# Building the count matrices of a graph network: five groups per comparison, from PSUM, with three places for the products

## The chip, the cores and the metric

The kernel runs on one core of a Trainium2 chip. The core has a matrix engine (TensorE, PE in the profile; PEld is its weight load), a vector engine (VectorE, DVE), a scalar engine (ScalarE, ACT), GpSimd (POOL, which here issues the gathers) and SyncE (SP, a queue of DMAs). Matrix products land in PSUM, which has eight banks of 2 KB in each of 128 partitions; all else is in SBUF. Every engine works through its own list in order and waits on semaphores of the others. The metric is the device time of one execution in microseconds.

## The reference

A three-layer graph convolution over 6250 nodes and 100,000 edges (sorted by target), with a residual connection and a layer norm. With self loops added,

```python
deg = segment_sum(1, dst);  dinv = rsqrt(deg)
for W, b in ((W1, b1), (W2, b2), (W3, b3)):        # 256->512, 512->512, 512->256
    h = h @ W
    h = relu(segment_sum(h[src] * (dinv[src] * dinv[dst])[:, None], dst) + b)
return layernorm(x + h)
```

The sum over edges is what costs: it is a product with a sparse 6250 x 6250 matrix of counts.

## The kernel before

Nodes come in 50 blocks of Q = 125. The aggregation of a layer is done block by block of targets, in one of two ways. A *gathered* block reads the rows of its sources from a table in DRAM, 16 chunks of 128 edges, one indirect DMA per chunk (`gather`, line 829, POOL). A one-hot matrix of the targets is compared on DVE, four chunks at a time, against the column numbers that lie in PSUM (`near_cols`, line 798), and a product with it adds the rows into an accumulator (`product`, line 855). Most rows are first split in two halves for a faster product: a cast on ACT (line 870), and the remainder on DVE (line 873). A *dense* block multiplies a 125 x 6250 matrix of edge counts, held as bytes, with the node features in SBUF (`parts`): pieces of it are converted by ACT or DVE (line 806) and go into 50 products (line 898).

Layer 0 takes blocks 0 to 17 dense and 18 to 49 gathered, layer 1 all 50 gathered, layer 2 blocks 0 to 27 dense and 28 to 49 gathered.

The count matrices are made by `counts` (line 688). A block of 125 targets has 25 groups of G = 5 targets, and each group has 128 slots of edges, whose source numbers within a block and keys (source block and target within the group) were laid out by `windows` in `slots`. For a group, DVE compares the 125 column numbers (line 702) and the 250 key numbers (line 704) with the slots' numbers, a product of both one-hot matrices counts the edges into 125 x 250 places of PSUM (`mat_ps`, line 710), and ACT evicts these as bytes into `made` (line 694), two steps and three steps after the comparisons. `mat_ps` is one bank with two halves that take turns. After 25 groups the matrix is stored from `made` to `kept` in DRAM (line 713, by `by_rows`, line 52), and a dense block fetches it from there later (line 720, by line 54). In layer 0 `making_few` makes a matrix and orders its fetch, one matrix after another, 18 in all; layer 1 makes the other ten, spaced 74 chunks apart, each by a generator of its own.

The order of the work is written out by hand. `layer` runs over the chunks. In each it issues the gather, the cast, the remainder and the product of chunks some steps back (the remainder two chunks and the product four chunks behind the gather in layers 0 and 1), then one step of everything in `going` (the work after a block's sum), then one step of each extra generator (`go_fixed`: `windows`, `making_few`, `counts`), then as many dense products as are due. A `yield 1` in a generator means: the next step in the next chunk. The framework adds the semaphores. The gathers of layer 0 go round 19 row buffers (`first_rows[2:]` in `room`), and their targets come free when the product or the split has read them.

Of the kernel before, what the change touches and what calls it, by code (L numbers as in the profile page):

```python
# [21 lines left out]
P = 128  # L22
# [21 lines left out]

EVEN = Q // 16 * 16
# [12 lines left out]
def general_path(ctx: ExitStack, tc: tile.TileContext, x, flat, wts, load_w3, room, out):  # L58
# [9 lines left out]
    w1_sb, w2_sb, w3_sb, b1, b2_sb, b3_sb = wts  # L68
# [22 lines left out]
    nc.scalar.dma_start(out=b1_sb, in_=bass.AP(tensor=b1.tensor, offset=b1.offset, ap=[[0, P], [1, HID]]))  # L91
    agg = const.tile([P, NB, HID], F32, name="agg")
# [280 lines left out]
def sorted_path(ctx: ExitStack, tc: tile.TileContext, x, edges, starts, found, wts, biases, room, late, out):  # L373
# [15 lines left out]
    w1_sb, w2_sb, w3_sb, b3_sb = wts  # L389
    b1, b2_sb = biases  # L390
# [21 lines left out]
    slots = const.tile([P, NW, 2, Q], F32, name="slots")  # L412
# [6 lines left out]
    thr0 = const.tile([P, Q], F32, name="thr0")  # L419
# [5 lines left out]
    def windows(t):  # L425
# [6 lines left out]
        nc.vector.tensor_single_scalar(thr, thr0, float(G * Q * t), op=ALU.add)  # L432
# [58 lines left out]
    with tc.tile_pool(name="sdeg1", bufs=1) as dp1, tc.tile_pool(name="sdeg", bufs=2) as dp, \  # L491
# [25 lines left out]
        thr_i = dp1.tile([P, Q], I32, name="sthr_i")  # L517
# [4 lines left out]
        def numbers():  # L522
# [4 lines left out]
            nc.gpsimd.iota(thr_i, pattern=[[G, Q]], base=0, channel_multiplier=0)  # L527
# [86 lines left out]
        with tc.manual_schedule():  # L614
# [13 lines left out]
            nc.vector.tensor_copy(thr0, thr_i)  # L628
# [20 lines left out]
    made, *used = [room[:Q, n * MW:(n + 1) * MW].bitcast(U8)[:, :NB * Q].rearrange("p (k v) -> p k v", v=Q) for n in range(3)]  # L649
    first_rows = [room[:, at:at + C] for at in range(3 * MW, room.shape[1] - C + 1, C)]  # L650
# [11 lines left out]
    pairs = early.enter_context(tc.tile_pool(name="spairs", bufs=4))  # L662
# [9 lines left out]
    near_cols = ps_cols.tile([P, 512], F32, name="near_cols")[:, :Q]  # L672
    nc.vector.tensor_copy(near_cols, cols[:, :Q])
# [14 lines left out]
    def counts(b, rush=GB + 3):  # L688

        def moved(u):
            nc.scalar.copy(made[:, :, u * G:(u + 1) * G],  # L694
                           mat_ps[:Q, u % 2, :G * NB].rearrange("p (k r) -> p k r", r=G))

        hot = {}
        for u in range(GB + 3):
            if u < GB:
                t, w = divmod(b * GB + u, Q)  # L700
                hot_lo = pairs.tile([P, Q], BF16, name="hot_lo")
                nc.vector.tensor_scalar(hot_lo, hot_cols[:, :Q], slots[:, t, 0, w:w + 1], None, op0=ALU.is_equal)  # L702
                hot_key = pairs.tile([P, G * NB], BF16, name="hot_key")
                nc.vector.tensor_scalar(hot_key, keys, slots[:, t, 1, w:w + 1], None, op0=ALU.is_equal)  # L704
                hot[u] = hot_lo, hot_key
            if u > 2:
                moved(u - 3)
            if 1 < u < GB + 2:
                hot_lo, hot_key = hot.pop(u - 2)
                nc.tensor.matmul(mat_ps[:Q, u % 2, :G * NB], lhsT=hot_lo, rhs=hot_key, start=True, stop=True)  # L710
            if u % rush != rush - 1:
                yield 1
        by_rows(nc.sync, made.rearrange("p k v -> p (k v)"), kept[b], store=True)
# [3 lines left out]
    finished = 0  # L717

# [4 lines left out]
    hot_cols = keys  # L723
# [12 lines left out]
    def layer(i, width, gathered, dense, after, rows, first=0, spacing=1.0, extras=()):  # L736
# [55 lines left out]
        def more_hots():  # L792
            c0 = len(hots) * HOTS
            n = min(HOTS, len(gathered) * (KF + 1) - c0)
            if n > 0:
                at = gathered[0] * (KF + 1) + c0
                hot = onehot.tile([P, HOTS, Q], F32R, name="shot")
                nc.vector.tensor_tensor(hot[:, :n], near_cols.unsqueeze(1).to_broadcast([P, n, Q]),  # L798
# [260 lines left out]
    def making_few():  # L1059

        for m, b in enumerate(few):
            while (b + 1) * GB > seen * Q:
                yield 1
            yield from counts(b) if m else counts(b, 2)
            while finished < m - 1:
                yield 1
            fetch(b, now + 10)

    first = 28
    spacing = (steps(FEW) - first - 12) / FEW  # L1070
    layer(0, C, every[FEW:], few, after1, first_rows, first, spacing, [(0, all_windows()), (1, making_few())])

    def last_weights():
        load_w2()
# [200 lines left out]
```

## Time and profile before

| | us |
|---|---|
| median of 3 runs | 2779.82 (2773.82 to 2794.7) |
| profiled execution | 2769.12 |
| its span | 2767.1 |
| PE busy in the span | 2130.1 (77%) |
| POOL | 1685.0 (61%) |
| DVE | 1512.0 (55%) |
| ACT | 1266.9 (46%) |

The mean granted clock of TensorE was 0.905 of full speed. The busy time of PE is modelled from the starts of its instructions, so 77% is not 77% of its peak. A row of the groups names the line, the engine, the operation, the tile written and those read, the shapes and the number of instructions, then their busy time, the mean of one in ns, and the engine's idle time just before them with what ended most of it. In a timeline the columns are start, duration, engine, line and operation, and in brackets the idle time before and its releaser. "remote" stands for a releaser that the profile cannot name. The durations of one execution are read against that execution; the median of the runs lies 10.7 us above it.

### The profile page before, as it was taken

What the parts mean: (1) busy time and instruction counts of PE and PEld (TensorE: products, weight loads), DVE (VectorE), ACT (ScalarE), POOL (GpSimd) and SP (SyncE); (2) the same over time, 40 slices, a digit from 0 to 9 for tenths busy, and PEclk for the clock granted to TensorE, in tenths of its full rate; (3) what the DMA queues carried; (4) which work ended last, traced back from release to release, by engine and by line L of the source; (5) the groups of instructions that cost most, each with busy time, mean ns of one, the idle gap of its engine ahead of it and who ended that gap; (6) DMA issues with size and microseconds to landing.
All of it is one profiled execution on the core that took longest, in us unless ns stands there. A gap on an engine that the chain in (4) does not pass through costs nothing.

```text
span 2767.1 us, 30455 instructions
## 1 busy us (share of the span) xinstructions
PE 2130.1 (77%) x7965; PEld 1459.2 (53%) x7965; DVE 1512.0 (55%) x3904; ACT 1266.9 (46%) x2777; POOL 1685.0 (61%) x1717
## 2 busy tenths in 40 slices
PE   3367678887878767878778878778787688888886
PEld 2245445555555434545555545545454466666664
DVE  5555445555555355555555555555554255655656
ACT  2445445555555344444444444444444244444443
POOL 2355556666666466667767667676676366566663
PEclk9988889999999888989998889999899789999998
DMA  7344445455445466666767667676676355555553
GB/s 174 92 124 115 134 136 146 123 149 148 126 143 143 123 196 194 203 195 201 211 191 211 186 181 216 195 203 201 182 216 198 98 137 150 142 147 153 151 145 93
DMA packets 178089, 447.70 MB, mean 162 GB/s; under 512 B 43347, under 2 KB 75429, under 8 KB 177904
## 3 DMA queue, kind: packets, MB, share of 16 engines
q0 software_dynamic: 107456, 326.24, 42.1%
q1 hardware_dynamic: 55328, 107.63, 13.5%
q10 hardware_dynamic: 15120, 11.77, 1.7%
q8 instruction: 65, 1.06, 0.2%
q14 instruction: 120, 0.98, 0.1%
HBM read 391.61 MB, written 53.88 MB: 161 GB/s over the span
## 4 chain that ended last, share of the span: by engine, by line
PE 53%; issue 17%; DVE 9%; another core or an unknown queue 7%; ACT 6%; DMA 5%; POOL 3%; ACTq 0%; POOLq 0%; SPq 0%; DVEq 0%
PE sacc L855 20%; PE sacc L898 10%; PE win_ps L985 5%; DMA room<-tab,ssrc 4%; PE win_ps L898 4%; PE mat_ps L898 3%; PE mat_ps L710 3%; PE smm L945 3%; DVE halves L873 3%; ACT halves L870 3%; POOL room L829 2%; PE smm L1002 2%; DVE shot L798 1%; ACT piece L806 1%
## 5 line engine op out<-in xcount | busy, mean ns | idle before, releaser
L829 POOL DMA_INDIRECT room<-tab,ssrc x1664 | 1650.0, 992 | 878.8 <-issue 333.3
L873 DVE TENSOR_TENSOR halves<-room,halves 128x256 fp32r<-128x256 f32 (+1 forms) x1208 | 663.6, 556 | 805.1 <-ACT halves L870 382.7
L855 PE MATMUL sacc<-halves,shot 128*125 128x512 f32 x1808 | 773.3, 486 | 156.0 <-issue 66.0
L870 ACT CAST halves<-room 128x256 fp32r<-128x256 f32 (+1 forms) x1208 | 600.9, 510 | 610.9 <-PE sacc L855 170.0
L855 PEld LDWEIGHTS sacc<-halves,shot 128*125 128x125 f32 x1808 | 349.4, 203 | 494.1 <-issue 289.1
L694 ACT CAST room<-mat_ps 125x250 uint8<-125x250 f32 x700 | 305.6, 437 | 544.2 <-PE mat_ps L710 165.4
L898 PE MATMUL sacc<-parts,piece 125*125 125x512 f32 x1400 | 498.7, 454 | 34.5 <-ACT piece L806 19.4
L855 PE MATMUL sacc<-room,shot 128*125 128x256 f32 (+1 forms) x1120 | 483.9, 516 | 10.6 <-DMA room<-tab,ssrc 10.6
L710 PE MATMUL mat_ps<-hot_key,hot_lo 128*125 128x250 bf16 x700 | 203.4, 291 | 308.3 <-issue 128.5
L898 PEld LDWEIGHTS sacc<-parts,piece 125*125 125x125 f32 x1400 | 254.8, 203 | 274.0 <-issue 196.4
L702 DVE TENSOR_SCALAR hot_lo<-keys,slots 128x125 bf16<-128x125 bf16 x700 | 193.6, 277 | 264.9 <-remote 114.2
L798 DVE TENSOR_TENSOR shot<-near_cols,sdlo 128x500 fp32r<-128x500 f32 x443 | 296.3, 669 | 0.1
L806 ACT CAST piece<-room 125x625 fp32r<-125x625 uint8 x376 | 264.9, 712 | 59.5 <-DVE halves L873 13.0
L855 PEld LDWEIGHTS sacc<-room,shot 128*125 128x125 f32 x1120 | 218.7, 204 | 130.0 <-issue 69.8
L985 PE MATMUL win_ps<-room,w_sb 128*128 128x250 f32 x800 | 218.2, 399 | 6.0 <-ACT room L993 5.3
L704 DVE TENSOR_SCALAR hot_key<-keys,slots 128x250 bf16<-128x250 bf16 x700 | 208.1, 297 | 0.0
L985 PEld LDWEIGHTS win_ps<-room,w_sb 128*128 128x128 f32 x800 | 164.7, 206 | 58.1 <-issue 26.1
L898 PE MATMUL mat_ps<-parts,piece 125*125 125x512 f32 x450 | 132.2, 412 | 16.9 <-ACT piece L806 8.4
L898 PE MATMUL win_ps<-parts,piece 125*125 125x512 f32 x450 | 134.1, 419 | 13.5 <-ACT piece L806 10.3
L710 PEld LDWEIGHTS <-hot_lo 128*125 128x125 bf16 x700 | 104.5, 150 | 60.9 <-issue 24.2
L945 PE MATMUL smm<-w,szt 128*125 128x512 f32 x200 | 110.6, 641 | 1.3 <-DVE st L950 0.6
L1002 PE MATMUL smm<-w,room 128*125 128x256 f32 x400 | 109.0, 398 | 0.0
(174 smaller groups left out, 1246.8 us busy)
## 6 DMA issues: line engine op xcount, KB each, us to landing
room<-kept SPq DMA_DIRECT2D x46, 683.6 KB
room<-tab,ssrc POOLq DMA_INDIRECT x1664
kept<-room SPq DMA_DIRECT2D x28, 683.6 KB
tab<-st SPq DMA_DIRECT2D x75, 224.0 KB
room<-tab SPq DMA_DIRECT2D x50, 224.0 KB
room<-in_x SPq DMA_DIRECT2D x50, 112.0 KB
out<-st ACTq DMA_DIRECT2D x50, 112.0 KB
room<-in_x ACTq DMA_DIRECT2D x4, 1120.0 KB
```

Source lines behind the costliest of these rows:

```text
L694: nc.scalar.copy(made[:, :, u * G:(u + 1) * G], mat_ps[:Q, u % 2, :G * NB].rearrange("p (k r) -> p k r", r=G))
L704: nc.vector.tensor_scalar(hot_key, keys, slots[:, t, 1, w:w + 1], None, op0=ALU.is_equal)
L710: nc.tensor.matmul(mat_ps[:Q, u % 2, :G * NB], lhsT=hot_lo, rhs=hot_key, start=True, stop=True)
L798: nc.vector.tensor_tensor(hot[:, :n], near_cols.unsqueeze(1).to_broadcast([P, n, Q]), dlo.rearrange("p b j -> p (b j)")[:, at:at + n].unsq ...
L806: convert(piece, used[m % 2][:, c * PIECE:(c + 1) * PIECE, :])
L829: nc.gpsimd.indirect_dma_start(out=row, out_offset=None, in_=tables[i], in_offset=bass.IndirectOffsetOnAxis(ap=at, axis=0))
L855: nc.tensor.matmul(acc[:Q, :size], lhsT=hot, rhs=row[:, c0:c0 + size], start=(i == 1 and k == c0 == 0), stop=(k == KF and c0 + size == row ...
L870: nc.scalar.copy(halves[:, :width], landed[chunk - hi_lag])
L873: nc.vector.tensor_sub(halves[:, width:], landed.pop(chunk - lo_lag), halves[:, :width].bitcast(F32))
L898: nc.tensor.matmul(acc_d[:Q], lhsT=got[done // PIECE][:, k % PIECE, :], rhs=parts[:, k], start=False, stop=(k == NB - 1))
L945: nc.tensor.matmul(y_ps, lhsT=zt[:, k, :], rhs=w1_sb[:, k, :], start=(k == 0), stop=(k == KC - 1))
L985: nc.tensor.matmul(h_ps[:, f, :], lhsT=w2_sb[:, k, (f2 + f) * P:(f2 + f + 1) * P], rhs=zt2[:, k, :], start=(k == 0), stop=(k == KH - 1))
```

## The change

`counts` now takes a list of blocks and a list of places, and runs over all their groups as one stream of steps. At every fifth step DVE compares the column numbers of five groups at once (625 elements) and the keys of three (750); two steps later it compares the keys of the other two (500). Both comparisons read the key numbers from PSUM: the tile `near_cols` now holds 250 numbers, of which line 798 still reads the first 125. The product of a group comes at step m + 4 and the eviction at m + 5; within a step the product now stands ahead of the eviction. Products go round three places: the two halves of `mat_ps`, and columns 256 to 505 of the bank of `near_cols`. In layer 0 all 18 matrices are one stream, at two steps a chunk for the first 25 steps, and their evictions go to `made` and `also_made` by turns; fetching is a generator of its own (`fetching_few`), behind `counts` in each chunk. The ten matrices of layer 1 have the one place `made` as before.

To make room, `also_made` is taken from the row buffers of layer 0 (13 are left in turn, of 19), `slots` is kept in bf16, `thr0` is gone (its numbers are computed from `cols` in one instruction, as before), and b3 is no longer loaded at the start but after layer 1, by a DMA in SP's queue.

```diff
-    slots = const.tile([P, NW, 2, Q], F32, name="slots")
+    slots = const.tile([P, NW, 2, Q], BF16, name="slots")
...
-        nc.vector.tensor_single_scalar(thr, thr0, float(G * Q * t), op=ALU.add)
+        nc.vector.tensor_scalar(thr, cols[:, :Q], float(G), float(G * Q * t), op0=ALU.mult, op1=ALU.add)
...
-    made, *used = [room[:Q, n * MW:(n + 1) * MW].bitcast(U8)[...] for n in range(3)]
-    first_rows = [room[:, at:at + C] for at in range(3 * MW, room.shape[1] - C + 1, C)]
+    made, *used, also_made = [room[:Q, n * MW:(n + 1) * MW].bitcast(U8)[...] for n in range(4)]
+    first_rows = [room[:, at:at + C] for at in range(4 * MW, room.shape[1] - C + 1, C)]
...
-    pairs = early.enter_context(tc.tile_pool(name="spairs", bufs=4))
+    pairs = early.enter_context(tc.tile_pool(name="spairs", bufs=2))
...
-    near_cols = ps_cols.tile([P, 512], F32, name="near_cols")[:, :Q]
-    nc.vector.tensor_copy(near_cols, cols[:, :Q])
+    near = ps_cols.tile([P, 512], F32, name="near_cols")
+    near_cols = near[:, :G * NB]
+    nc.vector.tensor_copy(near_cols, keys)
+    mat_places = [mat_ps[:Q, 0, :G * NB], mat_ps[:Q, 1, :G * NB], near[:Q, 256:256 + G * NB]]
...
-    def counts(b, rush=GB + 3):
-        def moved(u):
-            nc.scalar.copy(made[:, :, u * G:(u + 1) * G],
-                           mat_ps[:Q, u % 2, :G * NB].rearrange("p (k r) -> p k r", r=G))
+    def counts(blocks, places, rush=0):
+        def compared(out, numbers):
+            shape = list(out.shape)
+            nc.vector.tensor_tensor(out, near_cols[:, :shape[2]].unsqueeze(1).to_broadcast(shape),
+                                    numbers.unsqueeze(2).to_broadcast(shape), op=ALU.is_equal)
 
         hot = {}
-        for u in range(GB + 3):
-            if u < GB:
-                t, w = divmod(b * GB + u, Q)
-                hot_lo = pairs.tile([P, Q], BF16, name="hot_lo")
-                nc.vector.tensor_scalar(hot_lo, hot_cols[:, :Q], slots[:, t, 0, w:w + 1], None, op0=ALU.is_equal)
-                hot_key = pairs.tile([P, G * NB], BF16, name="hot_key")
-                nc.vector.tensor_scalar(hot_key, keys, slots[:, t, 1, w:w + 1], None, op0=ALU.is_equal)
-                hot[u] = hot_lo, hot_key
-            if u > 2:
-                moved(u - 3)
-            if 1 < u < GB + 2:
-                hot_lo, hot_key = hot.pop(u - 2)
-                nc.tensor.matmul(mat_ps[:Q, u % 2, :G * NB], lhsT=hot_lo, rhs=hot_key, start=True, stop=True)
-            if u % rush != rush - 1:
-                yield 1
-        by_rows(nc.sync, made.rearrange("p k v -> p (k v)"), kept[b], store=True)
+        total = len(blocks) * GB
+        for s in range(total + 5):
+            if s < total and s % GB == 0:
+                while (blocks[s // GB] + 1) * GB > seen * Q:
+                    yield 1
+            if s < total and s % WIDE == 0:
+                t, w = divmod(blocks[s // GB] * GB + s % GB, Q)
+                hot_lo = pairs.tile([P, WIDE, Q], BF16, name="hot_lo")
+                hot_key = pairs.tile([P, WIDE, G * NB], BF16, name="hot_key")
+                hot[s // WIDE] = hot_lo, hot_key
+                compared(hot_lo, slots[:, t, 0, w:w + WIDE])
+                compared(hot_key[:, :3], slots[:, t, 1, w:w + 3])
+            if s < total and s % WIDE == 2:
+                t, w = divmod(blocks[s // GB] * GB + s % GB + 1, Q)
+                compared(hot[s // WIDE][1][:, 3:], slots[:, t, 1, w:w + WIDE - 3])
+            m = s - 4
+            if 0 <= m < total:
+                hot_lo, hot_key = [h[:, m % WIDE] for h in hot[m // WIDE]]
+                nc.tensor.matmul(mat_places[m % 3], lhsT=hot_lo, rhs=hot_key, start=True, stop=True)
+            m = s - 5
+            if 0 <= m:
+                n, u = divmod(m, GB)
+                place = places[n % len(places)]
+                nc.scalar.copy(place[:, :, u * G:(u + 1) * G], mat_places[m % 3].rearrange("p (k r) -> p k r", r=G))
+                if u == GB - 1:
+                    by_rows(nc.sync, place.rearrange("p k v -> p (k v)"), kept[blocks[n]], store=True)
+                    stored.append(blocks[n])
+            if s >= rush or s % 2:
+                yield 1
...
-    def making_few():
+    def fetching_few():
         for m, b in enumerate(few):
-            while (b + 1) * GB > seen * Q:
-                yield 1
-            yield from counts(b) if m else counts(b, 2)
-            while finished < m - 1:
+            while b not in stored or finished < m - 1:
                 yield 1
             fetch(b, now + 10)
...
-    layer(0, C, every[FEW:], few, after1, first_rows, first, spacing, [(0, all_windows()), (1, making_few())])
+    layer(0, C, every[FEW:], few, after1, first_rows, first, spacing, [(0, all_windows()), (1, counts(few, (made, also_made), GB)), (1, fetching_few())])
...
-          extras=[(5, last_weights())] + [(10 + gap * n, counts(b)) for n, b in enumerate(many[FEW:])])
+          extras=[(5, last_weights())] + [(10 + gap * n, counts([b], (made,))) for n, b in enumerate(many[FEW:])])
     there.clear()
     fetch(many[0], 6)
     early.close()
+    b3_sb = ctx.enter_context(tc.tile_pool(name="slate_bias", bufs=1)).tile([P, C], F32, name="sb3")
+    nc.sync.dma_start(out=b3_sb, in_=bass.AP(tensor=b3.tensor, offset=b3.offset, ap=[[0, P], [1, C]]))
```

## The prediction

> **What bounds the kernel now.** I read the windows by stage first, since the three layers have different limits (layer 0 97 to 950 us, layer 1 953 to 2185, layer 2 2185 to 2767). Columns: stretch, length, then PE, PEld, DVE, ACT, POOL busy, granted clock, DMA share, GB/s.
>
> ```profile
> 97.00:950.00 853.00, 652.72 (x2572) 451.62 (x2572) 445.01 (x1476) 431.62 (x1041) 504.34 (x520) 0.91 0.46 130
> 953.00:2185.00 1232.00, 964.91 (x3351) 620.60 (x3351) 679.07 (x1413) 539.55 (x1075) 819.36 (x806) 0.90 0.68 195
> 2185.00:2767.00 582.00, 479.99 (x1845) 360.83 (x1845) 335.18 (x879) 262.56 (x598) 345.26 (x355) 0.91 0.52 138
> ```
>
> PE leads everywhere, and in layer 0 it idles 853.0 - 652.7 = 200 us. The groups of that stage say before which instruction:
>
> ```profile
> L710 PE MATMUL mat_ps<-hot_key,hot_lo 128*125 128x250 bf16 x450 | 130.9, 291 | 177.9 <-issue 60.8 <-DVE hot_key L704 53.5 <-ACT room L694 45.0
> ```
>
> 177.9 of the 200 us lie before L710, the counting product that the change rewrites. The releasers named disagree, so I read the timeline of an ordinary stretch:
>
> ```profile
> 706.54 0.27 PE L710 MATMUL mat_ps<-hot_key,hot_lo 128*125 128x250 bf16 x1
> ...
> 706.84 0.44 ACT L694 CAST room<-mat_ps 125x250 uint8<-125x250 f32 x1 [0.35 <-issue]
> ...
> 707.34 0.27 PE L710 MATMUL mat_ps<-hot_key,hot_lo 128*125 128x250 bf16 x1
> ...
> 709.34 0.43 ACT L694 CAST room<-mat_ps 125x250 uint8<-125x250 f32 x1 [1.48 <-PE sacc L855]
> ...
> 709.82 0.27 PE L710 MATMUL mat_ps<-hot_key,hot_lo 128*125 128x250 bf16 x1 [1.31 <-issue]
> ```
>
> Each product starts 0.05 us after the eviction of the product before it ends (706.84 + 0.44 + 0.05 = 707.34; 709.34 + 0.43 + 0.05 = 709.82), though that eviction reads the other half of mat_ps. In all 449 pairs of layer 0 none starts earlier. So mat_ps acts as one place, and PE and ACT go in lockstep: product, eviction, product. Eviction and next product are issued in the same step, so PE has no slack for a late ACT. The second stall is at the end of a matrix:
>
> ```profile
> 279.68 0.43 ACT L694 CAST room<-mat_ps 125x250 uint8<-125x250 f32 x1 [3.27 <-PE sacc L855]
> ...
> 280.13 0.75 SPq L52 DMA_DIRECT2D kept<-room  x2
> ...
> 294.51 0.43 ACT L694 CAST room<-mat_ps 125x250 uint8<-125x250 f32 x1 [12.92 <-remote]
> ...
> 295.00 0.37 PE L710 MATMUL mat_ps<-hot_key,hot_lo 128*125 128x250 bf16 x1 [13.85 <-DVE hot_key L704]
> ```
>
> The next matrix's first eviction waits until the store of the last has left `made`, and PE stands 13.85 us (mostly 2 to 4 us elsewhere). Summed from the timeline: 58 us in layer 0 at the second product of a matrix, 118 us at 87 other products; of the 118, 38 us is in excess of 1.5 us a gap.
>
> Layer 1 by the same view, with counting, without, with, without:
>
> ```profile
> 1192.00:1234.80 42.80, 31.56 (x121) 20.32 (x119) 26.78 (x74) 22.02 (x51) 27.38 (x28) 0.92 0.62 175
> 1234.80:1305.90 71.10, 59.08 (x196) 37.17 (x196) 39.09 (x68) 28.86 (x53) 50.62 (x50) 0.93 0.73 214
> 1305.90:1344.10 38.20, 28.59 (x116) 18.78 (x115) 25.70 (x70) 22.29 (x49) 28.72 (x27) 0.96 0.70 201
> 1344.10:1411.30 67.20, 56.74 (x199) 37.89 (x199) 36.93 (x64) 29.06 (x54) 47.36 (x47) 0.90 0.71 206
> ```
>
> Per gather (POOL's count): 42.8/28 = 1.53 and 38.2/27 = 1.41 us with, 71.1/50 = 1.42 and 67.2/47 = 1.43 without. Over all ten matrices I find 1.59 against 1.44: 27 steps x 0.15 x 10 = 41 us is all that counting costs there.
>
> **The change, part by part.** *Comparisons.* Rows:
>
> ```profile
> L702 DVE TENSOR_SCALAR hot_lo<-keys,slots 128x125 bf16<-128x125 bf16 x700 | 193.6, 277 | 264.9 <-remote 114.2
> L798 DVE TENSOR_TENSOR shot<-near_cols,sdlo 128x500 fp32r<-128x500 f32 x443 | 296.3, 669 | 0.1
> L704 DVE TENSOR_SCALAR hot_key<-keys,slots 128x250 bf16<-128x250 bf16 x700 | 208.1, 297 | 0.0
> ```
>
> The old pair overlaps: 0.44 us from the first's start to the second's end in the timeline, so 2.2 us for five groups. The new ones are shaped like L798, 669 ns at 500 elements; with the 1260-element comparison of the setup (1464 ns) the slope is 1.05 ns. So 625 elements 0.80, 750 0.93, 500 0.67: 2.40 us. DVE gains 140 x 0.2 = 28 us of work. The Trainium skill (VectorE: DVE Perf Modes, the perf-mode tier table) speaks against this part: 16-bit single-source operations in SBUF run at 4x, a two-source one with a PSUM operand at 1x. By the page's cycle table the old pair costs about 0.22 us, 1.1 for five, and the new ones 2.3: 170 us more DVE work by the rule, 28 by the rows. I take the rows. DVE is busy 445 of 853 us, which hides either; uncovered, 28 us is the price. What isn't averaged away: 0.80 + 0.93 = 1.73 us now stand in one step ahead of later `halves`, which PE needs two chunks (3 us) later. Covered.
>
> *Lead and places.* Compared inputs are two to four steps old rather than two: no gain by itself. Products go to three places, two in the old bank and one in the bank of near_cols; product before eviction within a step. A product into the old bank now waits for an eviction issued a step earlier, 1.5 us of slack. Of the 118 us that leaves the 38 us of excess, so 80 us could go; but PE then meets the next late thing (`halves`, `piece`: layer 2, which has no counting, still idles 102 of 582 us). I take 40.
>
> *Two places for matrices.* The store has 25 steps (40 us) to finish. The 58 us go; I take 50, as some of it will surface in front of L855. Half-clock pieces of 3.4 us follow 11 of these stalls; without them PE saves 11 x 1.7 = 19 at most, I take 10. The store itself and the fetch behind it stay in SP's queue, ahead of the same stores of `tab`; nothing there moves but the load of b3, from the start to after layer 1, behind the first fetch and ahead of after3's loads: 0 to 3 us, I take 1.
>
> *The new wait.* The trace says a bank is one place; the Trainium skill (PSUM, Partial Sum Buffer: PSUM bank collisions raise a hardware error) says the same for any two engines, disjoint columns and reads included. By that rule the third place isn't free: every third product must wait for all DVE reads of near_cols issued before it (comparisons and L798), and these for it, as must ACT's eviction. Behind the waiting product stand PE's L898 and L855; behind a waiting comparison DVE's `halves`. No row shows it. Lower bound 0: DVE now finishes a step's comparisons 1.5 us (median) before the product of the same step. Upper bound: the DVE work of the same step in full, 1.73 us at one of five such products, 0.67 at another, L798's 0.67 at about a quarter: 0.66 us each, 99 us for 150 products in layer 0, 55 for 83 in layer 1. A gain is excluded: it only adds waits. I take a third, because DVE's median lead nearly covers the long pair: 33 and 18.
>
> *The rest.* Gather rows in layer 0 fall from 19 to 13. Layer 1 runs on 11 with rows twice as wide; POOL stands 128 us in layer 0 because it is a full 19 ahead. 0 to 15 us, I take 3. Setup loses an iota and a copy: -1. `slots` in bf16, `thr` from cols: same instructions, 0.
>
> Sum, layer 0: -40 - 50 - 10 + 33 + 3 = -64. Layer 1: of the 41 us the product itself needs some 6; of 35 I take -33, then + 18: -15. With b3 and setup 0: **-79 us**. The profiled execution took 2769.1 (span 2767.1), so 2690; it lies 11 below the median of 2779.8, so against the median: **2701 us**.
>
> **The rivals.** (1) *Only the store stall goes* (0.17): the lockstep with ACT is replaced by one with DVE of the same cost; -58 to -30, about 2740. For it: no bank is spare. Against: only every third product meets DVE. (2) *The bank of near_cols decides* (0.17), slower: PE, DVE and ACT chained through it, `halves` behind comparisons that wait for PE, PE's L855 behind these. It outweighs the gain of about 133 us (100 in layer 0, 33 in layer 1) from 133/233 = 0.57 us for each third product; at 0.8 us it gives +53, about 2833. For it: the upper bound of 0.66 counts only one step's DVE work. Against: DVE's idle half. (3) *No change* (0.11), 2780: the late completions before the evictions (709.34, where ACT and DVE alike were waiting for PE) belong to PE itself and move to L855, and the store gain is eaten by (2). (4) *Forecast* (0.55), 2640 to 2750.
>
> **How the numbers follow.** A difference of 1% (28 us) is about what this kernel's measurement tells from none. Faster 0.55 + 0.17 = 0.72, same 0.11, slower 0.17. Low end 2645: all of the 80 and 58, the clock's 19, layer 1's 35, half the coupling taken: -135. High end 2800: it takes in no change and the milder part of (2). The forecast's own range is 2645 to 2750.
>
> **What would show it.** Right: idle before the counting product in layer 0 falls from 178 to under 90 us; no eviction waits for a store; layer 0 shortens by some 65 us, layer 1 by some 15; comparisons near 0.80, 0.93 and 0.67 us. Wrong: gaps of over 1 us before every third product, released by a comparison or L798; DVE idle before comparisons, released by L710; more idle before L855 for `halves`. A layer 0 that is no shorter with the gaps gone would mean PE's own late completions.

## The result and the profile after

| | before | after |
|---|---|---|
| median, measured side by side, us | 2784.9 (4 runs, 2773.82 to 2794.7) | 2747.05 (4 runs, 2741.93 to 2759.55) |
| profiled execution, us | 2769.12 | 2741.93 |
| its span, us | 2767.1 | 2740.3 |

The ratio is 0.985, with a 95% interval of 0.9806 to 0.9894: 38 us less, where 79 were forecast. The direction is as predicted, the size is not. The two profiled executions, which the windows and rows below come from, differ by 27 us.

The windows of the changed kernel by layer, columns as before (stretch, length, then PE, PEld, DVE, ACT, POOL busy, granted clock, DMA share, GB/s):

```profile
97.10:927.50 830.40, 641.88 (x2572) 440.47 (x2572) 462.48 (x847) 416.23 (x1041) 502.62 (x521) 0.90 0.47 134
927.50:2158.20 1230.70, 962.78 (x3351) 616.21 (x3351) 689.30 (x1063) 532.01 (x1075) 808.35 (x805) 0.90 0.67 195
2158.20:2740.30 582.10, 485.82 (x1845) 364.75 (x1845) 339.18 (x879) 263.46 (x598) 346.54 (x355) 0.90 0.52 138
```

In these two executions everything was gained in layer 0, 856 to 830 us (64 were forecast, 26 came). Layer 1 took 1231 us before and takes 1231 (15 were forecast). PE's idle time in layer 0, length less busy, went from 203 us (taken to 953 us) to 830.4 - 641.9 = 188.5: only 15 less, though the counting product lost far more. The groups of layer 0 in the changed kernel say where the rest is:

```profile
L963 PE MATMUL smm<-w,szt 128*125 128x512 f32 x200 | 110.0, 640 | 24.9 <-DVE st L968 15.7 <-DVE shot L816 5.4 <-DVE halves L891 2.7
L721 PE MATMUL mat_ps<-hot_key,hot_lo 128*125 128x250 bf16 x300 | 86.3, 290 | 35.3 <-ACT room L726 25.1 <-ACT halves L888 7.7 <-issue 2.4
L721 PE MATMUL near_cols<-hot_key,hot_lo 128*125 128x250 bf16 x150 | 45.9, 306 | 68.2 <-DVE hot_key L699 40.3 <-issue 15.6 <-DVE shot L816 5.8
L939 PE MATMUL szt_ps<-ident_r,szs 125*128 125x125 f32 x100 | 20.4, 286 | 17.1 <-ACT szt L957 9.2 <-issue 4.3 <-ACT piece L824 1.9
```

Two things are to be seen. The idle time before the counting product fell from 177.9 to 35.3 + 68.2 = 103.5 us, and two thirds of it now lie before the third of the products that go to the third place, with the long comparison as the releaser. And the products of `after1`, the work behind a block's sum (lines 963 and 939, before them 945 and 921), now wait 24.9 and 17.1 us, where they waited 1.3 and 2.1:

```profile
L945 PE MATMUL smm<-w,szt 128*125 128x512 f32 x200 | 110.6, 641 | 1.3 <-DVE st L950 0.6 <-ACT szt L939 0.5 <-issue 0.2
L921 PE MATMUL szt_ps<-ident_r,szs 125*128 125x125 f32 x100 | 19.6, 278 | 2.1 <-DVE szs L932 1.7 <-ACT szt L939 0.4
```

The executions fell into two settings of the hardware, whose cause the profile doesn't name: in one the kernel before took 2763 to 2785 us in median (A; "the first chip" of the expectations), in the other 2351 to 2352 us (B, "the second chip"), so ratios are compared within a setting only; the result above and the profile that the prediction read are of A.

### The profile page after: what moved, and what is told of

The parts are those of the page before. It is cut to its first block, busy times and chain, and to the rows that moved or that the text cites. A ratio compares the mean times of both kernels' runs of the same rounds, so it can differ in the third digit from the quotient of the medians.

```text
span 2740.3 us, 29549 instructions
## 1 busy us (share of the span) xinstructions
PE 2122.7 (77%) x7965; PEld 1447.4 (53%) x7965; DVE 1543.6 (56%) x2923; ACT 1245.0 (45%) x2777; POOL 1673.3 (61%) x1716
## 3 DMA queue, kind: packets, MB, share of 16 engines
q8 instruction: 65, 1.06, 0.2%
## 4 chain that ended last, share of the span: by engine, by line
PE 47%; issue 16%; DVE 8%; ACT 6%; another core or an unknown queue 5%; DMA 3%; POOL 2%; ACTq 0%; SPq 0%; DVEq 0%; POOLq 0%
PE sacc L873 19%; PE sacc L916 9%; PE win_ps L1003 4%; PE win_ps L916 3%; PE mat_ps L916 3%; ACT halves L888 3%; DMA room<-tab,ssrc 3%; DVE halves L891 3%; PE smm L1020 2%; PE smm L963 2%; DVE hot_key L699 2%; POOL room L847 2%; DVE shot L816 1%; ACT piece L824 1%
## 5 line engine op out<-in xcount | busy, mean ns | idle before, releaser
L916 PE MATMUL sacc<-parts,piece 125*125 125x512 f32 x1400 | 505.3, 453 | 40.6 <-ACT piece L824 19.3
L726 ACT CAST room<-mat_ps 125x250 uint8<-125x250 f32 x470 | 197.2, 436 | 304.8 <-PE mat_ps L721 119.6
L699 DVE TENSOR_TENSOR hot_key<-near_cols,slots 128x750 bf16<-128x750 f32 (+1 forms) x280 | 224.1, 801 | 37.9 <-remote 16.1
L726 ACT CAST room<-near_cols 125x250 uint8<-125x250 f32 x230 | 100.7, 438 | 197.3 <-DVE hot_key L699 65.3
L721 PE MATMUL mat_ps<-hot_key,hot_lo 128*125 128x250 bf16 x470 | 134.4, 288 | 68.6 <-ACT room L726 35.8
L721 PE MATMUL near_cols<-hot_key,hot_lo 128*125 128x250 bf16 x230 | 70.2, 305 | 140.4 <-DVE hot_key L699 62.8
L699 DVE TENSOR_TENSOR hot_lo<-near_cols,slots 128x625 bf16<-128x625 f32 x140 | 113.1, 808 | 54.3 <-PE sacc L873 14.6
```

The lines of the kernel that those rows point to most:

```text
L699: nc.vector.tensor_tensor(out, near_cols[:, :shape[2]].unsqueeze(1).to_broadcast(shape), numbers.unsqueeze(2).to_broadcast(shape), op=ALU. ...
L721: nc.tensor.matmul(mat_places[m % 3], lhsT=hot_lo, rhs=hot_key, start=True, stop=True)
L726: nc.scalar.copy(place[:, :, u * G:(u + 1) * G], mat_places[m % 3].rearrange("p (k r) -> p k r", r=G))
L916: nc.tensor.matmul(acc_d[:Q], lhsT=got[done // PIECE][:, k % PIECE, :], rhs=parts[:, k], start=False, stop=(k == NB - 1))
```

## The experiments

### The same two kernels again

No edit.

> The kernel before unaltered, for a profile on the same chip. Idle before its counting product: with the second matrix place alone it was 47 us in layer 0 and 69 us in layer 1; the store stall should add 17 gaps of 2 to 5 us, so 80 to 120 us in layer 0, if the second place is worth anything; 55 if the stall is covered.

> The changed kernel unaltered, so that it can be set beside the experiments on their chip (where the kernel before takes 2352 us, not 2785, and products complete without the late releases). The forecast's mechanism (waits removed before the counting product, less the new wait in the bank of near_cols) says a ratio of 0.97 to 0.99 here too. If the bank of near_cols costs what two places alone saved, it is slower than the kernel with two places (0.9897): 1.00 to 1.03.

> The changed kernel unaltered, beside the three below on one chip. Two chips have served so far: on one the kernel before takes about 2770 to 2785 us, on the other 2352. On the first a ratio of 0.9855 again. On the second, where products complete without late releases and the lockstep with ACT costs less: 0.99-1.02, since the bank of near_cols costs the same and there is less to gain; above 0.9897, the ratio of the kernel with two places there.

In A the changed kernel again took 0.9855 of the time before (0.9816 to 0.9894; medians 2727.25 and 2767.09). By a second profile of each (the kernel before took 2770.11 us in it), layer 0 went from 857 to 821 us, layer 1 from 1229 to 1225. So two executions of one kernel differ by up to 10 us in a layer, and the gain is stable. In B the changed kernel is slower: 1.0046 (1.003 to 1.0062; 2363.72 against 2350.95). A change that gains 1.5% in one setting and loses 0.5% in the other holds terms of both signs. The next runs take them apart.

### The second place for matrices, taken away

```diff
-    (1, counts(few, (made, also_made), GB))
+    (1, counts(few, (made,), GB))
```

> The changed kernel, but all matrices of layer 0 are evicted to the one place made. Theory (the store of the last matrix held the first eviction of the next, 58 us of idle before the product in layer 0, and the second place is the larger part of the gain): 2780-2800, gaps of 2 to 5 us back at the start of each of 17 matrices. Rival (with the places and the lead a store of 5 us is mostly covered): 2747-2760.

> The changed kernel with the one place made in layer 0, as e2. On the second chip 1.04 again. On the first: if the second place is worth the 50 us of the prediction, 1.003 (0.9855 + 0.018); if the stall without it grows to 6 us and more at each of 17 matrices because PE, DVE and ACT all hang on the bank, 1.02 or more.

> The changed kernel with the one place made in layer 0, a third time; wanted on the first chip. There: 1.003 if the second place is worth the predicted 50 us within the changed kernel; 1.02 or more if PE, DVE and ACT all hang on the bank of near_cols while the eviction waits for the store. On the second chip 1.04 again.

In A: 1.0023 (0.9994 to 1.0053), layer 0 back at 858 us. All the rest of the change together is worth nothing there. In B: 1.0395 (1.0372 to 1.0418) and 1.0379 (1.0348 to 1.041). The waits of layer 0 (columns: sum, number, longest, in us) show ACT's eviction waiting for the store again, in the run in A

```profile
ACT room L726 <- DMA kept<-room: 74.7, 15, 9.3
```

and in the second of those in B:

```profile
ACT room L726 <- DMA kept<-room: 82.0, 17, 9.5
```

The changed kernel with both places has no such row. Layer 0 of the second run in B, and of the changed kernel in B:

```profile
96.80:886.10 789.30, 630.08 (x2572) 436.31 (x2572) 461.64 (x847) 417.37 (x1041) 501.77 (x521) 0.92 0.48 141
96.80:809.10 712.30, 607.23 (x2572) 419.63 (x2572) 460.75 (x847) 417.02 (x1041) 504.18 (x520) 0.97 0.53 156
```

It grew by 789 - 712 = 77 us, about the 82.0 us of waiting. Not all of that is idle time of PE: 54 us are, and the other 23 are busy time of PE for the same instructions, at a granted clock of 0.92 instead of 0.97.

### The second place alone, put into the kernel before

```diff
-    made, *used = [... for n in range(3)]
-    first_rows = [room[:, at:at + C] for at in range(3 * MW, ...)]
+    made, *used, also_made = [... for n in range(4)]
+    first_rows = [room[:, at:at + C] for at in range(4 * MW, ...)]
...
-    def counts(b, rush=GB + 3):
+    def counts(b, rush=GB + 3, made=made):
...
-            yield from counts(b) if m else counts(b, 2)
+            yield from counts(b, made=(made, also_made)[m % 2]) if m else counts(b, 2)
```

> The kernel before with the second place for matrices in layer 0 alone (13 row buffers); comparisons, places of the products and their order as before. If the second place is worth what the prediction took (50 us): 2725-2745, and the changed kernel's other parts cancel. If the idle moves to other products: 2765-2785.

> The kernel before with the second place for matrices alone. On the first chip: the prediction took 50 us for it (0.982). On the second chip it gave 0.9967, so the stall of the store alone is mostly followed by another wait; if the same holds on the first chip, 0.99-1.00.

In A: 0.9889 (0.983 to 0.9948), layer 0 at 814 us, 43 less than before. By the ratio that is 31 us, most of the whole change's 38 to 40, for four edited lines. In B: 0.9967 (0.9953 to 0.998), 8 us. The counting product in layer 0 of this kernel, in A:

```profile
L710 PE MATMUL mat_ps<-hot_key,hot_lo 128*125 128x250 bf16 x450 | 131.0, 291 | 142.2 <-issue 60.0 <-ACT room L694 29.0 <-DVE hot_key L704 26.6
```

36 us of idle time before it went, and PE's idle time in the whole layer fell by nearly as much, 203 to 170 us (length less busy in the row below): this gain did not move elsewhere. PE's busy time fell too, from 653 us (in both profiled executions of the kernel before) to 643.

```profile
97.10:910.80 813.70, 643.32 (x2572) 447.43 (x2572) 443.88 (x1476) 431.77 (x1041) 507.27 (x520) 0.92 0.48 137
```

The products of `after1` hardly waited in it:

```profile
L945 PE MATMUL smm<-w,szt 128*125 128x512 f32 x200 | 105.6, 614 | 2.4 <-DVE st L950 1.2 <-issue 0.6 <-ACT szt L939 0.5
L921 PE MATMUL szt_ps<-ident_r,szs 125*128 125x125 f32 x100 | 20.3, 286 | 1.5 <-DVE szs L932 1.1 <-ACT szt L939 0.2 <-issue 0.2
L842 PE MATMUL sacc<-parts,ident_r 125*125 125x512 f32 x32 | 14.9, 465 | 1.4 <-DVE szs L932 1.4
```

### The third place, taken away

```diff
-    mat_places = [mat_ps[:Q, 0, :G * NB], mat_ps[:Q, 1, :G * NB], near[:Q, 256:256 + G * NB]]
+    mat_places = [mat_ps[:Q, 0, :G * NB], mat_ps[:Q, 1, :G * NB]]
...
-                nc.tensor.matmul(mat_places[m % 3], ...)
+                nc.tensor.matmul(mat_places[m % 2], ...)
```

(and `m % 2` in the eviction).

> The changed kernel, but products take turns in the two halves of mat_ps alone; nothing is counted into the bank of near_cols. Theory A (the wait between PE and DVE in the bank of near_cols is what took the missing gain: 68 us before that product in layer 0, 72 us in layer 1): those waits vanish and do not come back elsewhere, layer 0 falls from 830 to 780-805 us, layer 1 by 10 to 30, the whole to 2690-2725. Rival B (DVE is late in any case, and PE would wait for it at another instruction): idle moves to L855 and the products after a block's sum, the whole within 10 us of the changed kernel's 2747. Rival C (three places are what gives the slack): idle before the product rises above the changed kernel's 103 us in layer 0, the whole above 2760.

> The changed kernel with the products in the two halves of mat_ps alone, as e1. On the first chip: with narrow comparisons two places cost 18 thousandths against three (0.9924 and 0.9742), because the slack of the third hides late releases; but here the long comparisons leave PE's path with the third place. If the wait in the bank of near_cols is the larger: 0.975-0.985, faster than the changed kernel; if the third place's slack is: 0.99-1.00. On the second chip 0.99 again.

> The kernel with two places and long comparisons, a third time; wanted on the first chip (the kernel before at about 2770). There: if the wait in the bank of near_cols is the larger cost, 0.975-0.985; if the slack of the third place against late releases is, 0.99-1.00. On the second chip 0.99 again.

In A: 0.9867 (0.9812 to 0.9923), the same as with three places. In B: 0.9897 (0.988 to 0.9913) and 0.9916 (0.9886 to 0.9946), against 1.0046 with three, measured beside the second of these: there the third place costs 2363.72 - 2332.17 = 31.5 us. Layer 0 in B with three places,

```profile
L721 PE MATMUL mat_ps<-hot_key,hot_lo 128*125 128x250 bf16 x300 | 83.7, 282 | 2.8 <-ACT room L726 2.7
L721 PE MATMUL near_cols<-hot_key,hot_lo 128*125 128x250 bf16 x150 | 44.5, 297 | 50.7 <-DVE hot_key L699 42.6 <-DVE shot L816 6.5 <-ACT room L726 0.8
```

and with two:

```profile
L721 PE MATMUL mat_ps<-hot_key,hot_lo 128*125 128x250 bf16 x450 | 125.1, 278 | 21.7 <-ACT room L726 19.3
```

With three places the wait for ACT's eviction falls from 19.3 to 2.7 us. (That is not the third place's doing alone: with three places and the comparisons out of the bank, two sections on, it is 20.7.) In its stead come 50.7 us before the products of the third place, 49 of them released by DVE's reads of that bank. Layer 0 is 712 us with three places and 680 with two. The Trainium skill (PSUM, Partial Sum Buffer: PSUM bank collisions raise a hardware error) asks that two engines be kept apart by bank, not by column; the columns here are disjoint, and the products waited all the same. The waits are for semaphores, which the framework sets; no run here shows what the chip would do without them.

### Old comparisons with three places, and with two

The changed kernel with the comparisons of before, group by group from SBUF, but still four steps ahead; `slots` in F32, seven pairs of buffers:

```diff
-            if s < total and s % WIDE == 0:
+            if s < total:
...
-                compared(hot_lo, slots[:, t, 0, w:w + WIDE])
-                compared(hot_key[:, :3], slots[:, t, 1, w:w + 3])
...
+                nc.vector.tensor_scalar(hot_lo, keys[:, :Q], slots[:, t, 0, w:w + 1], None, op0=ALU.is_equal)
+                nc.vector.tensor_scalar(hot_key, keys, slots[:, t, 1, w:w + 1], None, op0=ALU.is_equal)
```

The kernel with two places has the edit of the section above as well.

> The changed kernel, but comparisons of one group at a time from SBUF as before (lines 702 and 704 of the kernel before; slots in float32), four steps ahead; three places, the third in the bank of near_cols. Theory A (long comparisons in the bank are what PE waits for): the third place's product now waits for L798's comparison alone, idle before it in layer 0 under 30 us, ratio 0.985-0.995. Rival (five groups at once save DVE time and so the wait): slower than the changed kernel.

> Narrow comparisons from SBUF, three places, as e5. On the first chip 0.974 again. On the second: if the long comparisons in the bank are the cost there too, faster than the changed kernel by 1% or more; if comparing five groups at once saves time there (DVE is busy 64% of the span), slower than the kernel with two places (0.9897).

> As e5, with the products in the two halves of mat_ps alone. If the gain of the two-place kernel (0.9897) comes from the lead and from the product standing ahead of the eviction, and not from comparing five groups at once: 0.985-0.993. If the comparisons from PSUM carry it: 0.995 or more.

In A: 0.9742 (0.9702 to 0.9782; 2697.92 us) with three places, 0.9924 (0.9891 to 0.9958; 2744.55 us) with two. In B, with three: 0.9926 (0.9897 to 0.9954). The four kernels that have both places for matrices, ratio to before in A (0.9867 has its own runs of the kernel before, the others share theirs):

| | two places for products | three |
|---|---|---|
| comparisons group by group, from SBUF | 0.9924 | 0.9742 |
| five groups at once, from PSUM | 0.9867 | 0.9855 |

With the old comparisons the third place is worth 2744.55 - 2697.92 = 47 us; with the long ones in its bank, by the ratios, 3 us, give or take 19. The long ones show no cost with two places (0.9867 against 0.9924), and cost 2727.25 - 2697.92 = 29 us with three (B: 2363.72 - 2334.16 = 30 us). So it is neither the comparisons' length nor the third place that costs, but that they meet in one bank. The kernel with old comparisons and three places beats both kernels of this case in both settings.

Its groups in layer 0, in A (lines lie three below those of the changed kernel, so 960, 936 and 857 are 963, 939 and 860 there):

```profile
L960 PE MATMUL smm<-w,szt 128*125 128x512 f32 x200 | 109.7, 638 | 14.2 <-DVE st L965 6.8 <-DVE shot L813 3.3 <-issue 2.2
L718 PE MATMUL mat_ps<-hot_key,hot_lo 128*125 128x250 bf16 x300 | 85.7, 288 | 61.3 <-ACT room L723 31.8 <-issue 22.5 <-ACT halves L885 5.4
L718 PE MATMUL near_cols<-hot_key,hot_lo 128*125 128x250 bf16 x150 | 43.2, 288 | 19.8 <-DVE shot L813 13.8 <-issue 5.2 <-ACT room L723 0.8
L936 PE MATMUL szt_ps<-ident_r,szs 125*128 125x125 f32 x100 | 20.9, 292 | 30.6 <-ACT szt L954 16.9 <-ACT halves L885 5.7 <-issue 3.8
L857 PE MATMUL sacc<-parts,ident_r 125*125 125x512 f32 x32 | 14.8, 462 | 14.2 <-DVE szs L947 10.2 <-issue 3.0 <-PE sacc L913 1.0
```

Its layer 0:

```profile
96.80:899.60 802.80, 631.57 (x2572) 440.09 (x2572) 430.70 (x1477) 413.03 (x1041) 507.37 (x521) 0.92 0.48 139
```

Here the long comparisons are gone, and yet PE's idle time in layer 0 is 802.8 - 631.6 = 171.2 us, as in the kernel before with the second place alone (813.7 - 643.3 = 170.4); the 11 us by which the layer is shorter lie in PE's busy time. Before the counting product it is 61.3 + 19.8 = 81.1 us instead of 142.2, so 61 us went; before the three other lines above it is 59.0 us, where that kernel had 2.4 + 1.5 + 1.4 = 5.3, so 54 us came back. Line 857, the first product into an accumulator, waits there for `after1` to have read the bank. By these sums lead and third place moved PE's waits in layer 0 to `after1`; they did not remove them. The sums don't say why `after1` is now late: PE may reach its products sooner, or the new order of steps may hold up its evictions, and no run changed `after1` alone.

The same is seen with long comparisons and two places, in A:

```profile
L721 PE MATMUL mat_ps<-hot_key,hot_lo 128*125 128x250 bf16 x450 | 128.8, 287 | 98.6 <-issue 50.7 <-ACT room L726 42.6 <-ACT halves L888 1.5
L963 PE MATMUL smm<-w,szt 128*125 128x512 f32 x200 | 110.0, 639 | 18.6 <-DVE st L968 11.8 <-issue 3.7 <-DVE halves L891 1.6
L860 PE MATMUL sacc<-parts,ident_r 125*125 125x512 f32 x32 | 14.6, 456 | 12.7 <-DVE szs L950 12.7
```

44 us less than 142.2 before the counting product, and layer 0 took 814 us, as with the second place alone.

### The long comparisons, but from SBUF

```diff
-            nc.vector.tensor_tensor(out, near_cols[:, :shape[2]].unsqueeze(1).to_broadcast(shape),
+            nc.vector.tensor_tensor(out, keys[:, :shape[2]].unsqueeze(1).to_broadcast(shape),
```

> The changed kernel, but the comparisons of five groups read the key numbers from SBUF (the tile keys, bf16), so of DVE only L798's comparison reads the bank of near_cols. Theory A: waits of the third place's product for hot_key vanish (63 us in both layers), the whole 2690-2725. Rival B: PE waits for the inputs or for halves instead, within 10 us of 2747. The duration of a comparison tells what the PSUM operand costs: near 0.8 us for 625 elements if only the element rate counts, about 0.45 if a 16-bit SBUF operand doubles it; if two SBUF inputs hold POOL up, POOL's gather grows beyond 984 ns.

1.0154 (1.0136 to 1.0172) in B, slower than the changed kernel there. The run was to free the bank and leave all else. It did free the bank of the long comparisons. Before the products of the third place in layer 0,

```profile
L721 PE MATMUL near_cols<-hot_key,hot_lo 128*125 128x250 bf16 x150 | 42.6, 284 | 20.5 <-DVE shot L816 15.3 <-ACT room L726 5.0
```

20.5 us of waiting are left of 50.7, and the 42.6 us that a comparison had ended are gone, though the comparisons are as long as before: that wait came from the bank, and not from the products' inputs. But the run did not leave all else. The products into `mat_ps` wait 21.0 us instead of 2.8. Two rows over the whole kernel, shapes kept apart,

```profile
L847 POOL DMA_INDIRECT room<-tab,ssrc x1664 | 1694.0, 1018 | 508.1 <-issue 225.1 <-DMA room<-tab,ssrc 82.0 <-DVE halves L891 53.3
L699 DVE TENSOR_TENSOR hot_lo<-keys,slots 128x625 bf16<-128x625 bf16 x140 | 113.2, 808 | 10.0 <-PE mat_ps L721 8.2 <-PE near_cols L721 1.7
```

and the gathers of the changed kernel in B:

```profile
L847 POOL DMA_INDIRECT room<-tab,ssrc x1664 | 1644.6, 988 | 538.0 <-issue 247.8 <-DMA room<-tab,ssrc 65.0 <-DVE halves L891 54.9
```

The comparisons hardly wait any more (10.0 us), but a gather takes 1018 ns instead of 988 (in layer 0, 1049 instead of 963). So this kernel's time doesn't tell the price of the bank, as another cost came in; the runs with two places do. Which of the new waits made it slower was not taken apart.

### Layer 1 with a fifth of its counting

```diff
-    def counts(blocks, places, rush=0):
+    def counts(blocks, places, rush=0, groups=None):
...
-            if s < total and s % WIDE == 0:
+            if s < total and s % WIDE == 0 and (groups is None or s < groups):
...
-          ... (10 + gap * n, counts([b], (made,)))
+          ... (10 + gap * n, counts([b], (made,), groups=5))
```

(and the same condition at the second comparison, the product and the eviction).

> The changed kernel; in layer 1, 20 of the 25 groups of each of the ten matrices are left out (no comparison, product or eviction; the store stays), so the counts of blocks 18 to 27 are not the graph's. What layer 1 pays for counting. If the 0.15 us a step of the prediction is on the path: layer 1 shorter by 25-40 us on the first chip, 5-10 on the second. If layer 1 is set by its gathers and splits, and slower steps while counting are made up for in between: under 10 us on both, as the idle before L873 grows by what goes before the product.

0.9799 (0.9728 to 0.987) in A. Layer 1 by its window:

```profile
921.80:2120.50 1198.70, 967.36 (x3151) 600.36 (x3151) 605.11 (x943) 475.32 (x875) 813.47 (x805) 0.90 0.69 201
```

1199 us, 26 to 32 less than the changed kernel's 1225 and 1231, for four fifths of the counting: all of it would cost 33 to 40 us. The medians of the whole kernel agree with that but don't pin it down: 0.9799 against 0.9855 is 16 us, give or take 22. The prediction had worked out 41 from the gathers' pace. So by the profiles there was about that much to gain in layer 1, and the change gained little or none of it (1231 and 1225 us, where it had been 1231 and 1229). Its own groups of layer 1 show why:

```profile
L873 PE MATMUL sacc<-halves,shot 128*125 128x512 f32 x1200 | 504.7, 509 | 143.5 <-ACT halves L888 73.5 <-issue 54.6 <-DVE halves L891 12.2
...
L721 PE MATMUL mat_ps<-hot_key,hot_lo 128*125 128x250 bf16 x170 | 48.1, 284 | 33.3 <-issue 15.4 <-ACT room L726 10.6 <-ACT halves L888 7.2
```

The 33.3 us before the products into `mat_ps` are joined by 72.2 us before the 80 into the third place: 105 together, where there were 130 before the change. And as much as left, and a little more, has come before line 873. The same two groups of layer 1 before the change:

```profile
L855 PE MATMUL sacc<-halves,shot 128*125 128x512 f32 x1200 | 507.3, 509 | 117.4 <-issue 64.6 <-ACT halves L870 36.4 <-DVE halves L873 9.2
...
L710 PE MATMUL mat_ps<-hot_key,hot_lo 128*125 128x250 bf16 x250 | 72.6, 290 | 130.4 <-issue 67.7 <-ACT room L694 21.8 <-DVE hot_key L704 21.7
```

With the counting nearly gone line 873 (874 in this kernel) waits longer still:

```profile
L874 PE MATMUL sacc<-halves,shot 128*125 128x512 f32 x1200 | 528.8, 521 | 195.4 <-ACT halves L889 85.9 <-issue 80.7 <-DVE halves L892 24.6
```

Of some 93 us of idle time taken from the counting product, 52 came back there.

## Why the prediction was half right

The runs in A split the time as the prediction split it (ratios times 2767 us):

| step | predicted, us | measured, us | by |
|---|---|---|---|
| second place for matrices, with the clock's part and the rows | -50 - 10 + 3 | -31 (interval -47 to -14) | put in alone; taken out: -47 |
| lead and places, layer 1's part with them | -40 - 33 | -41, give or take 20; -18 by the spans of the profiles | 0.9889 to 0.9742 |
| the wait in the bank of `near_cols` | +33 + 18 | +31, give or take 16 | 0.9742 to 0.9855 |
| sum | -79 (with b3 and setup at 0) | -41 | up to rounding the ratio 0.9855 itself, so it doesn't confirm the split; the first measurement gave -38 |

**The step that failed** is the size of the second row: 32 of the 39 us that are missing. (The first row is short by 26 us put in alone, by 10 taken out; the third cost 20 us less than allowed.) The prediction said of the lockstep's 118 us: "80 us could go; but PE then meets the next late thing (`halves`, `piece`: ...). I take 40", and of layer 1's 35: "I take -33". The direction of the first sentence was right, and half was still far too much. Without the long comparisons 61 us did leave the counting product in layer 0, and 54 returned before the next late thing. That was not `halves` or `piece` of that stage, but the products around `after1`, which wait for short evictions of ACT and DVE (`szt`, `st`, `szs`). By the profiles, layer 0 with old comparisons and three places is 11 us shorter than with the second place alone, and layer 1 12 us, against 40 and 33; what the medians gain beyond that (41 against 18 us) these two profiles don't show. That the measured 2747 us lie inside the forecast's own range of 2645 to 2750 is luck as far as this split goes.

**The new wait** has its sign, its place and its mechanism as predicted, and a size in time (31 of 51) within the bounds. Its idle time was larger than foreseen, 68.2 + 72.2 us instead of 33 + 18, and in layer 1 above the upper bound of 55; but much of that stands in the place of waits that PE had anyway. The gaps lie in the steps that were named: of the third-place products of layer 0 those of every fifth (the pair of 1.73 us) waited 0.93 us on average, another fifth (the 0.67 us comparison) 0.72 us, the other three fifths 0.21 us; in the second execution in A it was 0.73, 1.06 and 0.25. "DVE's median lead nearly covers the long pair" did not hold. The lead was read in a kernel in which DVE had nothing to wait for in that bank (and it is 1.3 us in median in that trace's layer 0, not 1.5); now the comparisons themselves wait for PE and ACT. The timeline of the changed kernel, where a pair and a third-place product share a step (rows of other work between them left out):

```profile
664.90 0.81 DVE L699 TENSOR_TENSOR hot_lo<-near_cols,slots 128x625 bf16<-128x625 f32 x1 [1.76 <-PE sacc L873]
665.62 0.93 DVE L699 TENSOR_TENSOR hot_key<-near_cols,slots 128x750 bf16<-128x750 f32 x1
...
666.61 0.32 PE L721 MATMUL near_cols<-hot_key,hot_lo 128*125 128x250 bf16 x1 [3.16 <-DVE hot_key L699]
```

The pair starts after 1.76 us of waiting for PE and ends at 665.62 + 0.93 = 666.55, and the product, whose own inputs were compared five steps earlier, starts 0.06 us later.

**The comparisons** cost what the rows had said, 0.80, 0.93 and 0.67 us predicted. By shape, in the changed kernel:

```profile
L699 DVE TENSOR_TENSOR hot_key<-near_cols,slots 128x750 bf16<-128x750 f32 x140 | 129.9, 928 | 0.0
L699 DVE TENSOR_TENSOR hot_lo<-near_cols,slots 128x625 bf16<-128x625 f32 x140 | 113.1, 808 | 54.3 <-PE sacc L873 14.6 <-ACT room L726 13.2 <-PE near_cols L721 9.8
...
L699 DVE TENSOR_TENSOR hot_key<-near_cols,slots 128x500 bf16<-128x500 f32 x140 | 94.2, 673 | 37.9 <-remote 16.1 <-ACT room L726 7.2 <-issue 4.0
```

DVE's busy time rose from 1512.0 to 1543.6 us, by 32 where 28 were predicted. The choice of the rows over the rule was right. The rule's estimate of 0.22 us for the old pair left out what the Trainium skill says beneath that cycle table (VectorE: DVE Perf Modes, The TRN2 errata), that the fixed part measures about 150 cycles and not 58: with that the estimate is 0.41 us, near the 0.44 of the trace.

**The second place** went as foreseen in its mechanism: no eviction waits for a store. The gain is 31 us alone to 47 within the change, against 57 with the clock's 10 and the rows' 3. The clock's part is borne out in kind: with the stalls gone PE's busy time in layer 0 fell from 653 to 643 us in A in the kernel before, and in B from 630 to 607 us in the changed kernel, as the granted clock rose from 0.92 to 0.97.

**The rivals.** The first (only the store's gain remains, 2740 us) comes nearest to the total in A: without the second place nothing is left (1.0023). Its reason is half right, since the lockstep's gain was lost to two things, the bank and `after1`. The second (the bank decides) is what happens in B: there the second place is worth 8 us put in alone, the lead and places another 10 (0.9967 to 0.9926), and the bank takes 30. It was not a matter of a higher price, but of less to gain. The third had PE's idle time move to line 855 and the gain be eaten; in layer 0 it moved to `after1` instead, in layer 1 26 us did move to that line, and the store's gain stayed.

**A sum that doesn't come out.** The low end of 2645 us rests on -135; its named parts give -80 - 58 - 19 - 35 = -192, and half of the coupling adds back 26 (of the 51 taken) or 77 (of the upper bounds of 99 and 55), not 57.

**What stays open.** The second place is worth 2439.19 - 2363.72 = 75 us in the changed kernel in B and 8 us in the kernel before. One reason may lie in the code: the stream reaches the next matrix's first eviction one step after the store, the old loop about three steps later. That was not tried. Nor was it tried to put the long comparisons and the third place into two different banks of PSUM.

## What to carry to other kernels

Free columns in a PSUM bank are not a free place: list who else touches that bank, in which step and for how long, and count a lead only if the change adds no wait to the engine that leads. Idle time before one product need not be a gain to be had (here 61 us left it and 54 came back elsewhere): PE's total idle time in the stage (length less busy), not one group's, shows whether a change removed it or moved it. Take out the stall with one named cause first (here a second buffer for a store, four lines); in the changed kernel in A it was the one gain that stayed.

## What the runs showed of the hardware

The kernel before took 2351 to 2352 us in one setting and 2763 to 2785 in the other, with a granted clock of 0.930 to 0.966 against 0.876 to 0.912 over its executions, and the durations of single gathers the same (988 and 984 ns for the changed kernel). The record has one chip number beside both settings, so the chip alone doesn't decide. What differs beside the clock is when PE's work is seen as done. In the kernel with the second place alone, 439 evictions in A found ACT idle (for over 0.1 us), and 129 of them began more than 0.5 us after the modelled end of their product (282 us in sum); in B it was none of 353. This would explain why slack behind PE, which the third place gives, is worth something in A and little in B; no run tested it alone.

A comparison with both inputs in SBUF as bf16 took 808 ns at 625 elements, and so did the same one with an input in PSUM as f32. The Trainium skill (VectorE: DVE Perf Modes, the perf-mode tier table) gives the former twice the rate of the latter, but on the condition that every tensor has a step of 1 or -1 (What auto-detection actually checks); here the slots' numbers are repeated along the row, a step of 0, and the two forms show no difference. The gathers beside the former took longer, 1018 ns instead of 988.
